# First attention of a decoder block: exponentials transposed by halves of the array, score strips read by 32 rows and 288 columns, contexts and side work spread over the steps

## Chip, cores and metric

The kernel runs on one NeuronCore of one Trainium2 chip. The metric is the device time of one execution in microseconds (us). Before the change three runs took 2130.73, 2132.78 and 2136.57 us; their median is 2132.78 us.

## What is computed

The reference is two transformer layers on x of 8 sequences x 512 tokens x 256 features, all in 32-bit floats: a disentangled attention with relative positions, a feed-forward layer with a low-rank part, a second attention over the sequences, and a mixture of 32 experts of which each token takes 4. Only the first attention is touched. It has 16 heads of 16 features:

```python
x = x + _L0_attn_ref(_layernorm(x))
...
scores = einsum('bhqd,bhkd->bhqk', q, k) / scale
c2p = take_along_axis(einsum('bhqd,hpd->bhqp', q, pos_k), clip(rel + 64, 0, 127))
p2c = swapaxes(take_along_axis(einsum('bhkd,hpd->bhkp', k, pos_k), clip(-rel + 64, 0, 127)))
probs = softmax(scores + (c2p + p2c) / scale)
ctx = einsum('bhqk,bhkd->bhqd', probs, v)
out = ctx @ Wo + bo + hidden
out = layernorm(out) * ln_scale + ln_bias
```

`rel` is a bucket of the distance between query and key. It changes only where the two are less than 128 tokens apart, so only a band of some 255 diagonals needs values of its own; outside the band the bucket is one of two constants.

## The kernel before

The first attention is the function `_l0_attention`. Its work is 256 steps: 8 sequences b, 4 groups g of four heads, 4 tiles i of 128 queries, and 2 pairs p of heads (L248). The order on every engine is the order in which the loop of L494 to L539 issues, since the schedule is manual (L486). One turn of the loop, for step n, does this:

- **Products** (L362). For both heads of the pair PE multiplies queries and keys into a score bank each (L371). A head has 16 features padded to 32 rows, so a matmul takes 32 rows of the array, and the matmuls of two heads stand in different row groups. There are two score banks, so a head's products wait until DVE has read the bank's last content.
- **Strips** (L306), for step n + 5 (`AHEAD`). PE multiplies 128 queries, and 128 keys, with the 256 possible positions of the band (L314), again in 32 rows. ACT copies the result to SBUF (L321). POOL works out what the tile's own 128 x 128 block needs beside it (`own`, L324). SP writes the strip, 4 x 128 rows of 255 values, to one of four DRAM buffers (L331). In the next turn SP reads it back with a row step of 511 values instead of 512, which shifts each row by one and turns positions into keys (`read`, L337 to L347): one transfer for the part by keys (`winp`), one for the part by queries (`winc`), each 128 partitions x 2 heads x 384 columns, or 256 where the tile is the first or last of the sequence. One turn later POOL adds `own` to the middle 128 columns of both (`add`, L351).
- **Near keys** (L379). PE transposes up to three 128 x 128 blocks of `winp` a head onto the scores (L383). Those of step n + 2 are the last that are needed.
- **Weights** (L393). DVE adds `winc` to the scores and takes each row's minimum (L397), and ACT makes the exponential (L400).
- **Turned** (L403). PE transposes the exponentials of step n - 1, four 128 x 128 blocks a head into one PSUM bank (L407), and DVE copies each bank to SBUF (L409).
- **Weigh** (L412), in every odd step. PE multiplies the transposed exponentials of four heads with the values: 16 matmuls, each of which is two instructions and takes 32 columns of the array (L418). After the last tile of an odd group ACT copies the contexts (L429), and `divide` is put in the list of side work.
- **Side work**: one piece a step. First what is `urgent`, the projections of the next group to queries and keys (L290); else the first of a list whose entries carry the first step in which they may run (`later`, L255): values (L273), normalizing and turning the next sequence (`normalized`, L152, and `turn`, L264), dividing (L447), and for the sequence before the output projection (`out`, L460), its mean and variance (`measure`, L469) and its normalization (`norm`, L472), which has twelve POOL operations of 256 columns (L475 to L477).

A transpose is a matmul whose stationary operand is the data, and whose moving operand is the identity. Every matmul of 32-bit floats that isn't a transpose shows as two instructions in the profile. The helper `_batch_norm_stats` (L47) takes mean and variance of a list of tiles on DVE (L53 to L56), and raises to the power -1/2 on POOL (L58). The lines named here are the ones that the prediction follows.

Of the kernel before, what the change touches and what calls it, by code (L numbers as in the profile page):

```python
# [12 lines left out]
F32 = mybir.dt.float32  # L13
# [8 lines left out]
P = 128  # L22
B, S, H = 8, 512, 256
# [37 lines left out]

def _normalize(nc, out, x, mv, rstd, i):
    nc.vector.tensor_scalar(out, x, mv[:, i, 0:1], rstd[:, i : i + 1], ALU.subtract, ALU.mult)  # L63


class _Evacuate:
# [24 lines left out]
def _l0_attention(nc, tc, a, x, ident, mhalf, carry, prefetch):  # L91
# [6 lines left out]
    with ExitStack() as ctx:  # L98
# [20 lines left out]
        with tc.tile_pool(name="a_pos", bufs=1) as pp:  # L119
# [32 lines left out]
            def normalized(pool, b):  # L152

                stats = []

                def measure():
                    stats.extend(_batch_norm_stats(nc, pool, [x[b][:, t, :] for t in range(NT)], 1e-5, mhalf))

                def norm():
                    for t in range(NT):  # L160
                        _normalize(nc, xns[b % 2][:, t, :], x[b][:, t, :], *stats, t)

                return measure, norm

            for f in normalized(pp, 0):
                f()


            def position_keys(lhsT, out):
# [61 lines left out]
        for v in vs:  # L231
            nc.gpsimd.memset(v, 0.0)

        winc = []
        for n in range(2 * NT):
            w = wp.tile([P, 2, S], F32, tag=f"winc{n}", name=f"winc{n}")
            nc.gpsimd.memset(w, 0.0)
            winc.append(w)

        ctx_ps = ps_c.tile([P, S], F32, tag="ctx", name="ctx_ps")  # L240

# [64 lines left out]
        def strips(u, between=None):  # L306


            b, g, i, p = steps[u]
            s = sm[b, g]  # L310
            pas = [ps_a.tile([P, S], F32, tag="psa", name="pa") for j in range(2)]
            for t, (src, pos) in enumerate(((s[0], posc), (s[2], posp))):
                for pa, rs in zip(pas, heads(p)):
                    nc.tensor.matmul(  # L314
                        pa[:, t * W : (t + 1) * W], src[rs, i * P : (i + 1) * P], pos[rs, g, :], start=True, stop=True
                    )
                if t == 0 and between is not None:
                    between()
            st = sb.tile([P, 4, W], F32, tag="strip", name="strip")
            for j in range(2):  # L320
                nc.scalar.copy(st[:, 2 * j : 2 * j + 2, :].rearrange("p t w -> p (t w)"), pas[j])  # L321

            own = sb.tile([P, 2, 2, P], F32, tag="own", name="own", bufs=3)
            nc.gpsimd.tensor_tensor(  # L324
                own,
                aside.unsqueeze(2).to_broadcast([P, 2, 2, P]),
                st[:, :, W - 1 : W].rearrange("p (j t) o -> p t j o", t=2).to_broadcast([P, 2, 2, P]),
                ALU.mult,
            )
            d = shift[u % NSHIFT]  # L330
            nc.sync.dma_start(  # L331
                bass.AP(d.tensor, d.offset + P + 1, [[2 * W, P], [2 * W * P, 4], [1, W - 1]]), st[:, :, : W - 1]
            )
            wc = winc[u % (2 * NT)]
            wk_ = sb.tile([P, 2, WIN], F32, tag="winp", name="winp", bufs=8)

            def read():  # L337
                lo, hi, c0, c1 = near(i)
                for t, dst in ((1, wk_[:, :, c0:c1]), (0, wc[:, :, lo * P : hi * P])):
                    nc.sync.dma_start(  # L340
                        dst,
                        bass.AP(
                            d.tensor,
                            d.offset + t * 2 * W * P + P + c0,
                            [[2 * W - 1, P], [4 * W * P, 2], [1, c1 - c0]],
                        ),
                    )  # L347
# [12 lines left out]
            wins[u] = wc, wk_  # L360
# [39 lines left out]
            nc.scalar.activation(e, e, AF.Exp, bias=low, scale=-1.0, accum_out=totals[b, g // 2][:, i, r : r + 1])  # L400
            return e

        def turned(e):  # L403
            et_ps = ps_t.tile([P, S], F32, tag="pst", name="et_ps")
            for m in range(NT):
                ms = slice(m * P, (m + 1) * P)
                nc.tensor.transpose(et_ps[:, ms], e[:, ms], ident)  # L407
            et = sb.tile([P, S], F32, tag="et", name="et", bufs=6)
            nc.vector.tensor_copy(et, et_ps)  # L409
            return et  # L410

        def weigh(n, ets):  # L412

            b, g, i, _ = steps[n]
            odd = g % 2 == 1
            for m in range(NT):
                for r, et in enumerate(ets):
                    nc.tensor.matmul(  # L418
                        ctx_ps[32 * r : 32 * r + 32, i * P : (i + 1) * P],
                        vs[b % 2][:, m, g % 2, g // 2 * 4 + r, :],  # L420
                        et[:, m * P : (m + 1) * P],
                        start=m == 0 and i == 0 and not odd,
                        stop=m == NT - 1 and odd,
                        skip_group_check=True,
                    )
            if i < NT - 1 or not odd:
                return
            c = sb.tile([P, S], F32, tag="c", name="c", bufs=2)
            nc.scalar.copy(c, ctx_ps)  # L429

            rec = sb.tile([P, NT, 8], F32, tag="rec", name="rec")
            nc.vector.reciprocal(rec, totals.pop((b, g // 2)))
            wide = sb.tile([P, NT, P], F32, tag="wide", name="wide", bufs=1)
            nc.gpsimd.tensor_copy(
                wide.rearrange("p i (r e) -> p i r e", e=HD), rec.unsqueeze(3).to_broadcast([P, NT, 8, HD])
            )
            later(3, partial(divide, b, c, wide))
            if g == NG - 1:
                out, measure, norm = finish(b)
                if b == B - 1:  # L440
                    rest.extend([*[partial(out, t) for t in range(NT)], measure, norm])
                else:
                    later(3, *[partial(out, t, misc, sb) for t in range(NT)])
                    later(9, partial(measure, misc, sb))
                    later(12, partial(norm, misc, sb))

        def divide(b, c, wide):  # L447
            spread = ps_m.tile([P, S], F32, tag="misc", name="spread")
# [6 lines left out]
        def finish(b):  # L455

            xn = xns[b % 2]
            stats = []

            def out(t, bank, pool):  # L460
                po = bank("po")
                for g in range(NC):
                    nc.tensor.matmul(
                        po[:, :H], cns[b][g][:, t * P : (t + 1) * P], wo[:, g, :], start=g == 0, stop=g == NC - 1
                    )
                nc.vector.tensor_tensor(xn[:, t, :], xn[:, t, :], po[:, :H], ALU.add)
                nc.gpsimd.tensor_tensor(xn[:, t, :], xn[:, t, :], rows["bo"], ALU.add)

            def measure(bank, pool):  # L469
                stats.extend(_batch_norm_stats(nc, pool, [xn[:, t, :] for t in range(NT)], 1e-7, mhalf))  # L470

            def norm(bank, pool):  # L472
                for t in range(NT):
                    _normalize(nc, xn[:, t, :], xn[:, t, :], *stats, t)
# [11 lines left out]
        with tc.manual_schedule():  # L486
# [7 lines left out]
            for now in range(len(steps) + 3):  # L494
                n = now
                if n < len(steps):
                    b, g, i, p = steps[n]
                    if (i, p) == (0, 0):
# [1176 lines left out]
```

## Time and profile before

| | us |
|---|---|
| median of three runs | 2132.78 |
| the profiled execution | 2132.52 |
| its span, from first to last instruction | 2130.7 |
| first attention, first product to the end of the last step | 56.1 to 1121.0 |
| PE, DVE, ACT, POOL busy over the span | 1963.5, 1393.8, 1104.7, 1138.3 |
| L407, transposes of exponentials, busy | 268.2 in 2048 instructions of 274 ns |
| L418, contexts, busy | 140.0 in 4096 instructions of 277 ns |
| L409, copies of the transposed, busy | 328.7 in 512 instructions of 683 ns |
| L397 and L400, minimum and exponential, busy | 333.2 and 365.7 |
| strip writes (L331) and reads (L340) | 256 of 510 KB, 256 of 384 KB, 256 of 256 KB |

In the profile, PE stands for matmuls and PEld for the loads of their stationary operands, which overlap with matmuls; SPq is the queue from which SP issues transfers. The ends of matmuls are modelled, so the distance between two starts says more than a duration. A line of the timeline gives start and length in us, then engine, line, operation and `out<-in`; in brackets stands how long the engine was idle before it, and what ended that. A name like `128*128 128x128` is the stationary operand's rows and columns, then the moving operand's.

### The profile page before, as it was taken

The numbers are of one execution on the slowest core, as the hardware profiler recorded it, in microseconds if no ns is written. First come the engines' busy times: TensorE is split into PE (matmuls) and PEld (weight loads), VectorE is DVE, ScalarE is ACT, GpSimd is POOL, SyncE is SP. The second block draws the span as 40 slices with busy tenths as digits, with TensorE's granted clock in tenths as the row PEclk, the third lists the DMA queues.
The fourth block names the chain that finished last, engine by engine and source line by source line (L and its number), as shares of the span: only waits on it lengthen the run. The fifth ranks groups of instructions, "written<-read, shape, count | busy, mean of one in ns | idle before, by whom it ended". The sixth has DMA issues, their size and how long they took to land.

```text
span 2130.7 us, 46004 instructions
## 1 busy us (share of the span) xinstructions
PE 1963.5 (92%) x15908; PEld 1415.5 (66%) x15908; DVE 1393.8 (65%) x3715; ACT 1104.7 (52%) x2366; POOL 1138.3 (53%) x1328
## 2 busy tenths in 40 slices
PE   7999999999999999999998999989988777499997
PEld 4777677777776777777775666645555445388886
DVE  3576776767767677686777555347876776356666
ACT  2776767667676766767662122244444333144443
POOL 5666766767667676676753111013544443355555
PEclk7999999999999999999999999999999987699999
DMA  8998989898898989989883544900111114556788
GB/s 273 316 293 275 283 278 299 271 290 282 269 299 276 277 280 282 295 270 293 275 283 93 165 142 126 87 0 29 46 40 43 49 42 167 198 166 209 253 259 268
DMA packets 388916, 444.21 MB, mean 208 GB/s; under 512 B 43344, under 2 KB 367952, under 8 KB 388688
## 3 DMA queue, kind: packets, MB, share of 16 engines
q1 hardware_dynamic: 373904, 401.93, 62.4%
q0 software_dynamic: 13824, 38.29, 4.9%
q8 instruction: 130, 2.13, 0.4%
q10 hardware_dynamic: 960, 1.05, 0.1%
q14 instruction: 98, 0.80, 0.1%
HBM read 238.99 MB, written 202.19 MB: 207 GB/s over the span
## 4 chain that ended last, share of the span: by engine, by line
PE 32%; DVE 10%; issue 4%; ACT 2%; SPq 1%; DMA 1%; POOL 1%; POOLq 0%; DVEq 0%; ACTq 0%
PE pge L1430 7%; PE po L674 5%; PE poe L1448 3%; PE ph L666 3%; PE pq L925 2%; PE ao L1015 2%; PE ptr L1422 2%; DVE prod L786 1%; PE pv L937 1%; DVE value L786 1%; PE po L1044 1%; SPq L1387 1%; PE ps L962 1%; DVE st L53 1%; DVE xn L63 1%
## 5 line engine op out<-in xcount | busy, mean ns | idle before, releaser
L397 DVE CUSTOM_DVE_ANT_0 e<-sc,winc 128x512 f32<-128x512 f32 x512 | 333.2, 688 | 293.9 <-PE sc L383 127.5
L400 ACT ACTIVATE e<-e,low 128x512 f32<-128x512 f32 x512 | 365.7, 716 | 110.1 <-DVE low L397 105.6
L324 POOL TENSOR_TENSOR own<-aside,strip 128x512 f32<-128x512 f32 x256 | 268.9, 1051 | 205.1 <-ACT strip L321 178.9
L321 ACT COPY strip<-pa 128x512 f32<-128x512 f32 x512 | 275.7, 592 | 185.7 <-issue 54.6
L371 PE MATMUL sc<-sm,sm 32*128 32x256 f32 (+3 forms) x1792 | 326.0, 439 | 19.2 <-DVE low L397 19.2
L409 DVE COPY et<-et_ps 128x512 f32<-128x512 f32 x512 | 328.7, 683 | 0.3 <-PE et_ps L407 0.2
L314 PE MATMUL pa<-pos,sm 32*128 32x256 f32 x2048 | 299.1, 407 | 1.7 <-ACT sm L298 1.0
L407 PE MATMUL et_ps<-ident,e 128*128 128x128 f32 x2048 | 268.2, 274 | 0.2 <-DVE et L409 0.2
L869 POOL DMA_INDIRECT rows<-pay,slot x128 | 141.9, 1109 | 233.0 <-issue 218.2
L371 PEld LDWEIGHTS sc<-sm,sm 32*128 32x128 f32 x1792 | 162.2, 184 | 130.3 <-DVE low L397 51.8
L407 PEld LDWEIGHTS et_ps<-ident,e 128*128 128x128 f32 x2048 | 234.3, 142 | 0.6 <-ACT e L400 0.4
L351 POOL TENSOR_TENSOR winp<-winp,own 128x256 f32<-128x256 f32 x256 | 186.9, 730 | 76.8 <-DMA winp<-shift 63.0
L869 POOL DMA_INDIRECT results<-y,r x160 | 156.8, 980 | 122.8 <-ACT y L1450 74.7
L351 POOL TENSOR_TENSOR winc<-winc,own 128x256 f32<-128x256 f32 x256 | 187.2, 731 | 40.0 <-DMA winc<-shift 37.4
L383 PE MATMUL sc<-ident,winp 128*128 128x128 f32 x1280 | 199.6, 285 | 5.8 <-DMA winp<-shift 5.8
L383 PEld LDWEIGHTS sc<-ident,winp 128*128 128x128 f32 x1280 | 136.4, 141 | 80.7 <-issue 59.6
L314 PEld LDWEIGHTS pa<-pos,sm 32*128 32x128 f32 x2048 | 179.8, 187 | 12.5 <-ACT strip L321 2.4
L58 POOL TENSOR_TENSOR rstd<-var,mhalf 128x4 f32<-128x4 f32 x40 | 44.8, 1121 | 249.3 <-DVE var L56 226.2
L1430 PE MATMUL pge<-store,rT 128*128 x640 | 168.2, 386 | 2.5 <-DVE rT L1424 0.9
L418 PE MATMUL ctx_ps<-et,v 128*32 128x128 f32 x4096 | 140.0, 277 | 0.2 <-DVE et L409 0.2
L669 ACT ACTIVATE hT<-ph,b 128x512 f32<-128x512 f32 x64 | 44.0, 687 | 166.0 <-PE ph L666 166.0
L290 PE MATMUL pq<-xnT,wqk 128*128 128x512 f32 x256 | 126.0, 614 | 3.1 <-DVE xnT L78 3.1
(216 smaller groups left out, 3337.3 us busy)
## 6 DMA issues: line engine op xcount, KB each, us to landing
shift<-strip SPq DMA_DIRECT2D x256, 510.0 KB
winp<-shift SPq DMA_DIRECT2D x128, 384.0 KB
winc<-shift SPq DMA_DIRECT2D x128, 384.0 KB
winp<-shift SPq DMA_DIRECT2D x128, 256.0 KB
winc<-shift SPq DMA_DIRECT2D x128, 256.0 KB
rows<-empty SPq DMA_DIRECT2D x8, 2640.0 KB
r<-rows SPq DMA_DIRECT2D x160, 132.0 KB
z<-results SPq DMA_DIRECT2D x32, 512.0 KB
```

The lines of the kernel that those rows point to most:

```text
L314: nc.tensor.matmul(pa[:, t * W : (t + 1) * W], src[rs, i * P : (i + 1) * P], pos[rs, g, :], start=True, stop=True)
L321: nc.scalar.copy(st[:, 2 * j : 2 * j + 2, :].rearrange("p t w -> p (t w)"), pas[j])
L324: nc.gpsimd.tensor_tensor(own, aside.unsqueeze(2).to_broadcast([P, 2, 2, P]), st[:, :, W - 1 : W].rearrange("p (j t) o -> p t j o", t=2).t ...
L351: nc.gpsimd.tensor_tensor(dst, dst, own[:, t], ALU.add)
L371: nc.tensor.matmul(sc[:, c0:c1], s[side_][rs, cut : cut + P], s[2 + side_][rs, c0:c1], start=c0 == 0, stop=False, skip_group_check=True,)
L383: nc.tensor.matmul(sc[:, m * P : (m + 1) * P], wins[n + 2 * (m - i)][1][:, j, (i - m + 1) * P : (i - m + 2) * P], ident, start=False, stop ...
L397: nc.vector.tensor_tensor_reduce(e, sc, wins[n][0][:, j, :], 1.0, -LOW, ALU.add, ALU.min, low)
L400: nc.scalar.activation(e, e, AF.Exp, bias=low, scale=-1.0, accum_out=totals[b, g // 2][:, i, r : r + 1])
L407: nc.tensor.transpose(et_ps[:, ms], e[:, ms], ident)
L409: nc.vector.tensor_copy(et, et_ps)
L869: ins = nc.gpsimd.indirect_dma_start(to, bass.IndirectOffsetOnAxis(ap=index, axis=0), source, None, bounds_check=last)
L1430: nc.tensor.matmul(pg[:, :H], rT[:, k * P : (k + 1) * P], w[:, k * H : (k + 1) * H], start=k == 0, stop=k == NK - 1)
```

## The change

It has four parts.

1. **Transposes by halves.** `turned` takes both heads of a step. Each 128 x 128 block of exponentials is transposed as two blocks of 64 rows, which take the upper and the lower half of the array's rows and go to two PSUM banks, in turn. Each of the two banks holds one half of the queries of both heads; DVE copies each bank as before. 8 transposes a step become 16, of 64 moving columns instead of 128.
2. **Strips read by 32 rows.** Each of the two reads becomes four, of 32 partitions. A row of the band needs only 255 columns, and 32 rows that are shifted against each other need 32 + 255, so each transfer reads 288 columns instead of 384 (fewer at the sequence's ends). The tiles that are read into are now permanent and cleared once at the start, since the columns outside the 288 have to stay zero; the tiles for `winc` of different query tiles share memory. The strip gets a third buffer.
3. **Contexts in every step.** `weigh` is done in two halves, half of the keys in an odd step and the other half in the even one after it.
4. **Side work in smaller pieces.** `measure` and `norm` handle two tiles at a time instead of four, and their pieces get earlier or other places in the list.

```diff
+def _measure(nc, pool, stats, tiles, eps, mhalf):
+    stats.append(_batch_norm_stats(nc, pool, tiles, eps, mhalf))
...
-                def measure():
-                    stats.extend(_batch_norm_stats(nc, pool, [x[b][:, t, :] for t in range(NT)], 1e-5, mhalf))
...
+                def measure(t):
+                    _measure(nc, pool, stats, [x[b][:, i, :] for i in (t, t + 1)], 1e-5, mhalf)
+
+                def norm(t):
+                    for i in range(2):
+                        _normalize(nc, xns[b % 2][:, t + i, :], x[b][:, t + i, :], *stats[t // 2], i)
+
+                return [partial(f, t) for f in (measure, norm) for t in (0, 2)]
...
+        winc, winp = [None] * (2 * NT), []
+        for p in range(2):
+            for i, width in ((0, S + 2 * P), (1, S + 3 * P)):
+                w = wp.tile([P, 2, width], F32, tag=f"winc{i}{p}", name="winc")
+                nc.gpsimd.memset(w, 0.0)
+                winc[2 * i + p], winc[2 * (NT - 1 - i) + p] = w[:, :, :S], w[:, :, width - S :]
         for n in range(2 * NT):
-            w = wp.tile([P, 2, S], F32, tag=f"winc{n}", name=f"winc{n}")
+            w = wp.tile([P, 2, WIN], F32, tag=f"winp{n}", name="winp")
             nc.gpsimd.memset(w, 0.0)
...
-            st = sb.tile([P, 4, W], F32, tag="strip", name="strip")
+            st = sb.tile([P, 4, W], F32, tag="strip", name="strip", bufs=3)
...
-            wk_ = sb.tile([P, 2, WIN], F32, tag="winp", name="winp", bufs=8)
+            wk_ = winp[u % (2 * NT)]
 
             def read():
-                lo, hi, c0, c1 = near(i)
-                for t, dst in ((1, wk_[:, :, c0:c1]), (0, wc[:, :, lo * P : hi * P])):
-                    nc.sync.dma_start(
-                        dst,
-                        bass.AP(
-                            d.tensor,
-                            d.offset + t * 2 * W * P + P + c0,
-                            [[2 * W - 1, P], [4 * W * P, 2], [1, c1 - c0]],
-                        ),
-                    )
+
+                lo, hi, first, end = near(i)
+                for t, dst, o in ((1, wk_, 0), (0, wc, (i - 1) * P)):
+                    for p0 in range(0, P, 32):
+                        c0, c1 = max(first, p0), min(end, p0 + 2 * P + 32)
+                        nc.sync.dma_start(
+                            dst[p0 : p0 + 32, :, o + c0 : o + c1],
+                            bass.AP(
+                                d.tensor,
+                                d.offset + t * 2 * W * P + P + c0 + p0 * (2 * W - 1),
+                                [[2 * W - 1, 32], [4 * W * P, 2], [1, c1 - c0]],
+                            ),
+                        )
...
-        def turned(e):
-            et_ps = ps_t.tile([P, S], F32, tag="pst", name="et_ps")
-            for m in range(NT):
-                ms = slice(m * P, (m + 1) * P)
-                nc.tensor.transpose(et_ps[:, ms], e[:, ms], ident)
-            et = sb.tile([P, S], F32, tag="et", name="et", bufs=6)
-            nc.vector.tensor_copy(et, et_ps)
-            return et
+        def turned(es):
+
+
+            banks = [ps_t.tile([P, S], F32, tag="pst", name="et_ps") for _ in range(2)]
+            for j, e in enumerate(es):
+                for m in range(NT):
+                    for f, bank in enumerate(banks):
+                        rs, c = slice(64 * f, 64 * f + 64), (j * NT + m) * 64
+                        nc.tensor.transpose(bank[:, c : c + 64], e[rs, m * P : (m + 1) * P], ident[rs, rs])
+            et = sb.tile([P, 2, 2, NT, 64], F32, tag="et", name="et", bufs=4)
+            for f, bank in enumerate(banks):
+                nc.vector.tensor_copy(et[:, f].rearrange("p j m q -> p (j m q)"), bank)
+            return [et[:, :, j] for j in range(2)]
...
-        def weigh(n, ets):
+        def weigh(n, ets, part):
...
-            for m in range(NT):
+            for m in range(2 * part, 2 * part + 2):
...
-                        et[:, m * P : (m + 1) * P],
+                        et[:, :, m, :],
...
-            if i < NT - 1 or not odd:
+            if part == 0 or i < NT - 1 or not odd:
                 return
-            c = sb.tile([P, S], F32, tag="c", name="c", bufs=2)
+            c = sb.tile([P, S], F32, tag="c", name="c", bufs=1)
...
+                fs = [*[partial(out, t) for t in range(NT)], *[partial(f, t) for f in (measure, norm) for t in (0, 2)]]
                 if b == B - 1:
-                    rest.extend([*[partial(out, t) for t in range(NT)], measure, norm])
+                    rest.extend(fs)
                 else:
-                    later(3, *[partial(out, t, misc, sb) for t in range(NT)])
-                    later(9, partial(measure, misc, sb))
-                    later(12, partial(norm, misc, sb))
+                    later(3, *[partial(f, misc, sb) for f in fs])
...
+                        if g == NG - 3 and b + 1 < B:
+                            ready = normalized(sb, b + 1)
+                            later(4, *ready[:2])
                         if g == NG - 2 and b + 1 < B:
-                            measure, norm = normalized(sb, b + 1)
-                            later(1, measure)
-                            later(3, norm, *[partial(turn, b + 1, k) for k in range(NK)])
+                            later(2, *ready[2:], *[partial(turn, b + 1, k) for k in range(NK)])
...
-                        ets.extend(turned(e) for e in es)
+                        ets.extend(turned(es))
...
-                    weigh(n - 3, [ets.popleft() for _ in range(4)])
+                    four = [ets.popleft() for _ in range(4)]
+                    weigh(n - 3, four, 0)
+                elif n % 2 == 0 and n >= 4:
+                    weigh(n - 4, four, 1)
```

`measure` and `norm` of the output get the same form in `finish`.

More of the change, by code (lines that the diff above doesn't have):

```diff
@@ L154, in normalized @@
                 stats = []
-                def measure():
-                    stats.extend(_batch_norm_stats(nc, pool, [x[b][:, t, :] for t in range(NT)], 1e-5, mhalf))
[L159 to L166, printed above, removed]
+                def measure(t):
[4 more added lines that the diff above has]
+                return [partial(f, t) for f in (measure, norm) for t in (0, 2)]
+            ready = normalized(pp, 0)
+            for n in (0, 2, 1, 3):
+                ready[n]()
             def position_keys(lhsT, out):
@@ L232, in _l0_attention @@
             nc.gpsimd.memset(v, 0.0)
-        winc = []
+        winc, winp = [None] * (2 * NT), []
[4 more added lines that the diff above has]
+                winc[2 * i + p], winc[2 * (NT - 1 - i) + p] = w[:, :, :S], w[:, :, width - S :]
         for n in range(2 * NT):
-            w = wp.tile([P, 2, S], F32, tag=f"winc{n}", name=f"winc{n}")
+            w = wp.tile([P, 2, WIN], F32, tag=f"winp{n}", name="winp")
             nc.gpsimd.memset(w, 0.0)
-            winc.append(w)
+            winp.append(w)
         ctx_ps = ps_c.tile([P, S], F32, tag="ctx", name="ctx_ps")
@@ L467, in out, with measure, norm @@
                 nc.gpsimd.tensor_tensor(xn[:, t, :], xn[:, t, :], rows["bo"], ALU.add)
[L469 to L474, printed above, removed]
+            def measure(t, bank, pool):
+                _measure(nc, pool, stats, [xn[:, i, :] for i in (t, t + 1)], 1e-7, mhalf)
+            def norm(first, bank, pool):
+                for t in (first, first + 1):
+                    _normalize(nc, xn[:, t, :], xn[:, t, :], *stats[first // 2], t - first)
                     nc.gpsimd.tensor_tensor(xn[:, t, :], xn[:, t, :], rows["ln_scale"], ALU.mult)
```

## Prediction

> **What bounds the kernel now.** I read the busy table by stage first, then the timeline of single steps, then the waits, then SP's own rows. The change touches the first attention alone: 256 steps between 56.1 and 1121.0 us of a 2130.7 us span, 4.16 us a step.
>
> ```profile
> core 0: us, PE busy (x) PEld busy (x) DVE busy (x) ACT busy (x) POOL busy (x), PEclk, DMA share, GB/s
> 56.10:1121.00 1064.90, 1035.77 (x11781) 774.47 (x11780) 752.08 (x1854) 738.53 (x1672) 725.79 (x902) 0.99 0.91 284
> ```
>
> PE is busy 97% of the stage, DVE, ACT and POOL about 70%; the DMA engines stand at 91%. The timeline of one step (time, us, engine, line, tiles) says what PE's time is made of:
>
> ```profile
> 603.98 0.19 PEld L371 LDWEIGHTS sc<-sm,sm 32*128 32x128 f32 x2 [0.20 <-issue]
> 603.99 0.19 PEld L314 LDWEIGHTS pa<-pos,sm 32*128 32x128 f32 x2
> ...
> 604.75 0.38 PE L314 MATMUL pa<-pos,sm 32*128 32x256 f32 x2
> 605.05 0.64 PEld L383 LDWEIGHTS sc<-ident,winp 128*128 128x128 f32 x6 [0.33 <-issue]
> 605.06 0.87 PE L383 MATMUL sc<-ident,winp 128*128 128x128 f32 x6
> ...
> 605.66 0.91 PEld L407 LDWEIGHTS et_ps<-ident,e 128*128 128x128 f32 x8
> 605.77 1.04 PE L407 MATMUL et_ps<-ident,e 128*128 128x128 f32 x8
> ```
>
> Four things are to be seen. (a) Eight transposes at L407 take 1.04 us, of which the last is 0.27: one starts every (1.04-0.27)/7 = 0.110 us. (b) Four loads of 32 rows, two at L371 and two at L314, start within 0.01 us and all last 0.19: loads in different row groups run side by side. (c) L383 to L407 costs nothing (605.06 + 6 x 0.109 = 605.71 against 605.77, the rest being the first load), but the last L314 pair starts at 604.75, needs 0.21 (its neighbours start 0.21 apart) and L383 starts only at 605.05: 0.09 us lost where the shape of the array changes. L407 to L418 (last start 602.77, +0.11, L418 at 602.97) and L418 to L371 show 0.09 too. (d) The two loads ahead of a first transpose, looked at alone:
>
> ```profile
> 605.05 0.20 PEld L383 LDWEIGHTS sc<-ident,winp 128*128 128x128 f32 x2 [0.33 <-issue]
> ```
>
> One lasts 0.14, two 0.20: a load in a transpose needs about 0.057 us, so today's 0.110 is set by the 128 columns of identity that stream, not by the load.
>
> ```profile
> PEld sc L371 <- DVE low L397: 51.8, 137, 1.4
> ...
> PE sc L371 <- DVE low L397: 19.2, 28, 1.2
> ```
>
> These waits (us, times, longest) are short steps that catch up with DVE: the next products need the score bank that DVE's L397 still reads. SP's rows (min/median/max ns):
>
> ```profile
> L340 SPq DMA_DIRECT2D winp<-shift x256: 359/447/1676, 44.5 to 1107.6; - x128
> L340 SPq DMA_DIRECT2D winc<-shift x256: 359/927/1522, 44.9 to 1108.1; - x128
> ...
> L599 SPq DMA_DIRECT2D token_rows<-xn x8: 319/324/338, 1104.6 to 1319.4; - x8
> ```
>
> An issue costs SP 0.36 us at least, and a 16-row one at L599 still 0.32: the cost hardly depends on the rows.
>
> **What the Trainium skill says.** "TensorE: Matmul & The Clock Gate", Part 3: weight loads overlap running matmuls only when the row group differs; the trace agrees (b). "TensorEngine Tiling (Array Packing)", Key Properties: a change of tiling mode drains the array; the trace agrees at 0.09 us. "SBUF — State Buffer", Door 1: partitions 0..31 reach 8 of 16 DMA ports and measured 189 GB/s; "DMA: Bandwidth & Descriptors", Rules for kernel authors: two transfers to disjoint partition halves serialize. No run here shows either; today's strip reads go to 128 partitions.
>
> **The change, part by part** (us a step; times 256 for the stage).
>
> Halved transposes. Removed: 8 x 0.109 = 0.87. Added: 16 of 64 rows and 64 columns. Streaming is 0.109/2 = 0.055; the load, still 128 columns, 0.057; the halves are two row groups and two banks, so 8 pairs x 0.057 = 0.46, plus a new change of shape after L383 (0.09) and its uncovered first load (0.055): 0.60. Net -0.27, -68 us. Bounds: streaming alone, 8 x 0.055, gives -0.28; no overlap, 16 x 0.057 + 0.15 = 1.06, gives +0.19. I take -0.27. DVE's two copies (L409, 0.68 each) are unchanged, and come after L397 in DVE's order anyway.
>
> Contexts by halves. The same 32 matmuls, in every step instead of every second. A step is quiet when no side work runs on PE in it. Odd quiet steps exceed even ones (2.75) by 1.01 where no wait is in them, of which 8 sets of four x 0.107 = 0.86 stream; entering costs about 0.14, now also in 128 even steps: +18. Where side work on PE follows in an even step, it now comes from another shape (today's steps from 85.44 to 89.70 and on to 95.16, both with a projection, differ by 5.46 - 4.26 = 1.20, about 0.20 more than the quiet ones): 20 of a batch's 32 steps have such work (8 projections, 4 values, 4 outputs, 2 divides, 2 turns), half of them even, 80 x 0.20 = +16.
>
> Evenness. Quiet steps today alternate 4.24 (from 97.91 to 102.15) and 2.75 (on to 104.91); 0.47 of the pair, 0.24 a step, is the wait for DVE. Afterwards a quiet step needs 2.75 - 0.27 + 0.43 + 0.14 = 3.05 of PE. But there is a loop: from the first near key (605.06) to the end of the second L397 2.09, 0.07 to the next products, 1.07 from there to the next near key: 3.23. PE work that is taken out of a quiet step below this only turns into that wait, so 0.18 of it stays; (0.24 - 0.18) x 96 quiet steps = -6.
>
> Measures and norms by halves. Steps with them run over today; against the sums of their PE work a batch loses about 5 us. What a norm issues stays: four L63 on DVE (0.72 to 0.78 each), for the output's norm also twelve POOL operations (L475 to L477, 0.74 each, 8.9 in all); each measure now makes two L58 on POOL, 1.1 each, instead of one. The halves follow each other in successive quiet steps, where POOL already has own and two adds, 2.5 of 3.2. So POOL catches up hardly sooner: behind the norm stand the next strip's own (L324) and the adds (L351), and the near keys wait for those. I take -1 a batch, -8; bounds 0 and -40.
>
> Reads. Bytes: today 768 KB inside and 512 at the edges, mean 640; after, 32 rows x 288 columns give 576, the clipped edges (mean 208 columns) 416, mean 496. With the 510 KB write that is 1.03 MB instead of 1.18; at 284/0.91 = 312 GB/s 3.3 us a step instead of 3.8. DMA isn't what PE waits for (L383 for DMA: 14 us in all), so this is worth about nothing directly. Price: 9 issues instead of 3. SP: 9 x 0.36 + 0.08 of semaphores = 3.3 us a step, under the mean step, 0.1 over a quiet one. Behind the eight reads stands the next strip's write; POOL's adds wait for four landings each instead of one, with the next own behind them, and the near keys two steps on wait for the adds. Strips run five steps ahead, so long steps pay back what SP loses in short ones: +4. PE's extra semaphore waits are hidden behind its queue, as two per step at L407 are now.
>
> Third strip buffer, persistent winp tiles, one c: 0, since ACT's strips start 0.09 us after PE's last L314 ends, and so wait for PE. POOL's memsets grow from 8 x 1024 to 12,800 elements a partition, at 0.95 us per 1024 by 4.3 us, in 9.8 us of POOL's idle time before 40.12; without that cover +4. The last half of the contexts comes one step later: +1.
>
> Sum: -68 + 18 + 16 - 6 - 8 + 4 + 1 = -43. The profiled execution took 2132.5 (span 2130.7 and 1.8 around it), 0.3 under the median of 2132.8; 2132.5 - 43 is **2090**.
>
> **Rivals.**
> (1) Slower: the **DMA engines become the bound**, since a 32-row read reaches half the ports. At the page's 189 GB/s the mean 0.51 MB of reads takes 2.69 us, the write 0.52 MB/312 = 1.67, semaphores 0.08: 4.44 against 4.16 now, +0.28 x 256 = +72: 2205. It decides from 4.16 - 1.75 = 2.41, i.e. reads under 211 GB/s. For: 91% today. Against: neighbouring reads alternate between port halves, and packets of several reads are in flight together.
> (2) **SP becomes the bound**: today's medians are 0.45 and 0.93, waiting for a full DMA queue. At 0.45 a step is 9 x 0.45 + 0.08 = 4.13, 0.03 under today: 2125. It decides from 0.43: 9 x 0.43 + 0.08 = 3.95 is about my mean step after (4.16 - 43/256 = 3.99).
> (3) The **halves don't overlap** (the change doesn't do what it says): (1.06 - 0.60) x 256 = 118 on the forecast, 2208. Against it is (b).
> (4) **More is won**: the bursts vanish (-32 more) and the lighter DMA takes away the few long stalls in which DVE stood for winp (28.4 us): 2030.
>
> **How the numbers follow.** Forecast 0.50, (1) 0.18, (2) 0.13, (3) 0.06, (4) 0.13. A measurement of this kernel tells about 0.3% from no change, 6 us. Forecast and (4) are faster, and half of (2); a third of (2) is within: faster 0.69, same 0.05, slower 0.26. The forecast's own range is 2062 (the bursts gone) to 2112 (half of the change's gain lost to SP). The wide range takes in (2), most of (4) and the milder half of (1), at which the halves are partly used together: 2045 to 2190; some 2 in 10 are left out, the rest of (1) and (4), and (3).
>
> **What would show it.** Right: L407 pairs every 0.057 us, 0.46 a step; 0.09 between L383 and L407; quiet steps of 3.2; L418 in every step; SP's read issues at 0.36. Wrong: L407 starts 0.057 apart one by one (3); SP's reads at 0.45 and more with PE's L383 waiting for winp (2); the DMA share over 0.95 with fewer GB/s (1). Any of these makes the forecast wrong.

## The result and the profile after

The changed kernel takes **2408.9 us** (2407.0 to 2411.7), against 2132.2 for the kernel before beside it: a ratio of 1.1295, 95% interval [1.1275, 1.1315]. The forecast was 2090 with a range of 2045 to 2190; the kernel became 277 us slower, and the sign was wrong. Its profiled span is 2406.8 us, and nearly all of the difference lies in the stage that the change touches. A step there now takes 5.24 us on average (from the first product of step 0 to that of step 255) instead of 4.16. First the same table of the stage as shown for the kernel before:

```profile
core 0: us, PE busy (x) PEld busy (x) DVE busy (x) ACT busy (x) POOL busy (x), PEclk, DMA share, GB/s
56.80:1397.00 1340.20, 1093.90 (x13805) 734.59 (x13804) 746.22 (x1867) 738.83 (x1672) 734.69 (x916) 0.90 0.74 198
```

PE was busy 97% of the stage and is now busy 82%; DVE, ACT and POOL do the same work in a longer time; the DMA engines have fallen from 91% to 74% and from 284 to 198 GB/s. So no engine of this table is the bound. The waits of the stage (us, times, longest) say what PE and POOL lack:

```profile
POOL winp L365 <- DMA winp<-shift: 238.3, 174, 6.1
PE sc L397 <- DMA winp<-shift: 234.5, 93, 9.3
```

The near keys (L397) and the adds (L365) wait for windows that haven't landed, while the DMA engines stand idle for a quarter of the time: the transfers come late because they are *asked for* late. Who asks is SP. Its timeline in the kernel before (start, us, line; x1 is one issue):

```profile
501.63 0.36 SPq L331 DMA_DIRECT2D shift<-strip  x1
502.09 0.45 SPq L340 DMA_DIRECT2D winp<-shift  x1
502.63 0.94 SPq L340 DMA_DIRECT2D winc<-shift  x1
505.39 0.36 SPq L331 DMA_DIRECT2D shift<-strip  x1
```

and in the changed kernel:

```profile
499.77 0.38 SPq L342 DMA_DIRECT2D shift<-strip  x1
500.25 2.38 SPq L354 DMA_DIRECT2D winp<-shift  x4
502.74 1.77 SPq L354 DMA_DIRECT2D winc<-shift  x4
504.61 0.38 SPq L342 DMA_DIRECT2D shift<-strip  x1
```

Before, SP issues for 1.9 us and then waits 1.8 us for the next strip. Now one issue follows the other without a pause, and the step is as long as the nine issues: 504.61 - 499.77 = 4.84 here. The rows of SP's reads, and its waits in the stage before and after, say the same:

```profile
SPq L331 <- ACT strip L321: 478.2, 249, 4.1
```

```profile
L354 SPq DMA_DIRECT2D winp<-shift x1024: 302/438/2500, 44.6 to 1384.0; - x171
L354 SPq DMA_DIRECT2D winc<-shift x1024: 302/425/2135, 46.4 to 1385.9; - x171
...
SPq L342 <- ACT strip L332: 9.1, 29, 0.9
```

SP used to wait 478 us for strips; now 9. (Each `x1024` row holds all reads into one of the two windows, four a step; its three numbers are the shortest, the median and the longest issue in ns.) The medians, 0.44 and 0.43, are not yet the whole price. Sorted by their place after the write (100 to 1000 us, mean us), the nine issues take 0.40 (the write), 0.46, **0.97**, 0.46, 0.43, 0.43, 0.51, 0.47 and 0.46, in sum 4.6; between them lie gaps of about 0.06, 0.52 a step, and the semaphore instructions take 0.07. Together 5.2 of a 5.26 us step: **SP is the bound.**

PE doesn't lose this time evenly. The 32 first steps of a group of heads (tile 0, first pair) last 383 us in sum, 12.1 in the median, where the kernel before takes 141 and 4.25: 242 of the 277 us that were lost lie there. The near keys of tile 3 need no window of a later tile, so PE works on while SP falls behind; the next tile 0 needs one that stands three further on in SP's order than any that PE has needed so far, and there PE has to wait until SP has caught up:

```profile
728.93 0.87 PE L397 MATMUL sc<-ident,winp 128*128 128x128 f32 x3 [5.48 <-DMA winp<-shift]
729.74 1.12 PE L425 MATMUL et_ps<-ident,e 64*128 64x64 f32 x16
```

The halved transposes themselves, by contrast, are as forecast (start, us):

```profile
504.33 0.63 PE L397 MATMUL sc<-ident,winp 128*128 128x128 f32 x4 [1.16 <-DMA winp<-shift]
504.89 0.71 PE L425 MATMUL et_ps<-ident,e 64*128 64x64 f32 x16
505.54 0.64 PE L437 MATMUL ctx_ps<-et,v 128*32 128x128 f32 x16
```

Sixteen take 0.65 from the first start to the first context, where eight took 0.96 to 0.97 (448.08 to 449.05 in the kernel before), and pairs start 0.06 apart. The bracket on the first line is a wait for a window, in the middle of a step.

### The profile page after: what moved, and what is told of

It reads as the page before. It is cut to its first block, busy times and chain, and to the rows that moved or that the text cites. A ratio compares the mean times of both kernels' runs of the same rounds, so it can differ in the third digit from the quotient of the medians.

```text
span 2406.8 us, 52429 instructions
## 1 busy us (share of the span) xinstructions
PE 2021.8 (84%) x17956; PEld 1377.3 (57%) x17956; DVE 1385.8 (58%) x3731; ACT 1104.9 (46%) x2366; POOL 1151.3 (48%) x1348
## 3 DMA queue, kind: packets, MB, share of 16 engines
q10 hardware_dynamic: 960, 1.05, 0.1%
## 4 chain that ended last, share of the span: by engine, by line
PE 32%; DVE 9%; SPq 6%; DMA 5%; issue 4%; POOL 2%; ACT 2%; another core or an unknown queue 0%; POOLq 0%; DVEq 0%; ACTq 0%
PE pge L1452 5%; PE po L696 5%; SPq L354 4%; DMA winp<-shift 3%; PE poe L1470 3%; PE ph L688 3%; PE ao L1037 1%; PE pq L947 1%; PE ptr L1444 1%; DVE prod L808 1%; PE sc L397 1%; PE sc L385 1%; PE et_ps L425 1%; PE ctx_ps L437 1%; PE pv L959 1%
## 5 line engine op out<-in xcount | busy, mean ns | idle before, releaser
L397 PE MATMUL sc<-ident,winp 128*128 128x128 f32 x1280 | 231.5, 302 | 234.8 <-DMA winp<-shift 234.5
L397 PEld LDWEIGHTS sc<-ident,winp 128*128 128x128 f32 x1280 | 144.5, 149 | 329.7 <-issue 190.4
L365 POOL TENSOR_TENSOR winp<-winp,own 128x256 f32<-128x256 f32 x256 | 185.7, 725 | 301.5 <-DMA winp<-shift 238.3
L365 POOL TENSOR_TENSOR winc<-winc,own 128x256 f32<-128x256 f32 x256 | 186.4, 728 | 254.6 <-DMA winc<-shift 221.8
L325 PE MATMUL pa<-pos,sm 32*128 32x256 f32 x2048 | 305.4, 417 | 1.7 <-ACT sm L309 1.0
L385 PEld LDWEIGHTS sc<-sm,sm 32*128 32x128 f32 x1792 | 167.6, 191 | 111.8 <-issue 47.9
L425 PE MATMUL et_ps<-ident,e 64*128 64x64 f32 x4096 | 199.6, 243 | 1.1 <-DVE et L428 1.1
L425 PEld LDWEIGHTS et_ps<-ident,e 64*128 64x128 f32 x4096 | 162.3, 151 | 50.6 <-issue 36.9
L437 PE MATMUL ctx_ps<-et,v 128*32 128x128 f32 x4096 | 184.6, 304 | 0.5 <-DVE et L428 0.5
L58 POOL TENSOR_TENSOR rstd<-var,mhalf 128x2 f32<-128x2 f32 (+1 forms) x56 | 51.2, 915 | 229.2 <-DVE var L56 207.1
L301 PE MATMUL pq<-xnT,wqk 128*128 128x512 f32 x256 | 158.2, 748 | 0.1
L309 ACT ACTIVATE sm<-pq,bias 128x512 f32<-128x512 f32 x128 | 80.8, 683 | 121.8 <-PE pq L301 115.3
```

Of the source, the lines that this page charges most:

```text
L325: nc.tensor.matmul(pa[:, t * W : (t + 1) * W], src[rs, i * P : (i + 1) * P], pos[rs, g, :], start=True, stop=True)
L385: nc.tensor.matmul(sc[:, c0:c1], s[side_][rs, cut : cut + P], s[2 + side_][rs, c0:c1], start=c0 == 0, stop=False, skip_group_check=True,)
L397: nc.tensor.matmul(sc[:, m * P : (m + 1) * P], wins[n + 2 * (m - i)][1][:, j, (i - m + 1) * P : (i - m + 2) * P], ident, start=False, stop ...
L425: nc.tensor.transpose(bank[:, c : c + 64], e[rs, m * P : (m + 1) * P], ident[rs, rs])
```

## The experiments

The theory after the result: the PE side of the forecast stands, and the loss is SP's issuing, at some 0.58 us an issue with its gap instead of the 0.36 forecast. The rival is the forecast's rival (1): not the issues cost the time, but the transfers themselves. All ratios are to the kernel before, run beside each kernel; a difference in us is the difference of ratios times 2132. E9 to E11 ran on another chip, where the kernel before took 2145.4 us, so only their ratios can be set beside the others. A transfer's *rows* are its contiguous pieces, one for each partition and head: 64 in a 32-partition read, 256 in a whole read, 512 in the write.

**E1, whole reads.** The changed kernel with the two reads of a step by all 128 rows again:

```diff
-                    for p0 in range(0, P, 32):
-                        c0, c1 = max(first, p0), min(end, p0 + 2 * P + 32)
-                        nc.sync.dma_start(
-                            dst[p0 : p0 + 32, :, o + c0 : o + c1],
...
+                    nc.sync.dma_start(
+                        dst[:, :, o + first : o + end],
```

> The changed kernel with its strip reads put back to one transfer of 128 rows each (384 columns, 256 at the ends), so SP issues 3 transfers a step instead of 9; halved transposes, split contexts and side work stay. Theory A (SP's issues are the bound of the changed kernel: 9 a step at 0.53 us and 0.06 between them are 5.2 us): SP falls to under 2 us a step, PE is the bound again, and what the prediction summed for the other parts is left, 2090 us (2070 to 2110). Theory B (32-row transfers are slow in the DMA engines[...]): also about 2090, since those are gone too. Theory C (the halved transposes or the order of side work cost the time): over 2200 us.

Measured: 2107.3 us, 0.9888 [0.9858, 0.9917]. Everything but the reads together gains 24 us; the reads cost 300. That the transfers themselves were slow isn't excluded by this run, since they are gone too. The stage's table is back to the form of before:

```profile
56.10:1094.00 1037.90, 1006.45 (x13806) 693.32 (x13805) 755.50 (x1868) 740.08 (x1673) 727.96 (x916) 1.00 0.93 291
```

**E2, reads by 64 rows.** As the change, with `range(0, P, 64)` and 320 columns: five issues a step.

> The changed kernel with reads of 64 rows and 320 columns: 4 reads a step instead of 8[...]. Theory A: SP issues 5 transfers, about 2.9 us a step, less than PE needs; 2090 to 2115 us. Theory B: [...]4.6 us a step, 2250 us or more.

Measured: 2129.9 us, 0.9994 [0.9973, 1.0014], a little above my range and far below theory B, which is the forecast's rival (1) again. Five issues don't cost five ninths: the reads of 64 partitions (128 rows) take 0.57 to 0.60 each in the median back to back where those of 32 partitions took 0.43. SP is at 3.8 of a 4.15 us step: just short of the bound.

**E3, six more issues.** The kernel before, with six transfers of 64 rows of four values each behind the reads, into tiles that nobody uses. They add 6 KB to a step's 1.2 MB:

```diff
+                for _ in range(6):
+                    spare = sb.tile([32, 2, 4], F32, tag="spare", name="spare", bufs=64)
+                    nc.sync.dma_start(
+                        spare, bass.AP(d.tensor, d.offset, [[2 * W - 1, 32], [4 * W * P, 2], [1, 4]])
+                    )
```

> The kernel before, with six transfers of 32 rows x 2 x 4 values (16 bytes each row) added on SP after the two reads of each step, into tiles that nothing reads. They add 6 KB a step, and no work elsewhere. Theory A: SP needs 1.7 us for what it does now, and 6 x 0.43 us and 0.06 between them more, 4.9 to 5.0 us a step against 4.16: 2320 us (2250 to 2400). Theory B: nothing but 6 KB more, 2132 to 2145 us.

Measured: 2452.3 us, 1.1503 [1.1475, 1.1531]. That is above even theory A's range: six issues that move next to nothing cost as much as the changed reads. The bytes aren't needed for such a loss. How much of it is SP's issuing this run alone doesn't say: E7 finds a second limit that holds it too.

**E4, the reads alone.** The kernel before with the 32-row reads and nothing else of the change.

> The kernel before with the reads by 32 rows and 288 columns alone (and the permanent winp tiles that they need); whole transposes, contexts in odd steps, two strip buffers. Theory A: SP's 5.2 us a step stay the bound, so about the changed kernel's time, 2400 us (2370 to 2450), the other parts hidden behind SP. Theory C: between 2132 and 2200, the loss being in the other parts.

Measured: 2394.0 us, 1.1234 [1.1205, 1.1263], as expected. Even on the slower PE side of the kernel before, SP sets the step: its issues, gaps and semaphore instructions are 5.17 of 5.20 us.

**E5, halved transposes alone.** The kernel before with `turned(es)` of the change.

> The kernel before with the transposes by halves alone; reads, contexts and side work as before. Theory A (the step costs what its TensorE work costs, and the halves save 0.27 us of it): 256 steps x 0.27 = 69 us less, 2064 us (2055 to 2080). Theory B (a saving on TensorE comes back as waits for the strips or in the bursts of side work): 2085 to 2110. If the halves had shared the array badly it would be above 2132.

Measured: 2123.1 us, 0.9952 [0.9936, 0.9969]: 10 us of the 69. Where the rest went can be read in one quiet pair of steps, the last two of a group. The kernel before:

```profile
447.59 0.66 PE L383 MATMUL sc<-ident,winp 128*128 128x128 f32 x4
448.08 1.04 PE L407 MATMUL et_ps<-ident,e 128*128 128x128 f32 x8
449.05 1.17 PE L371 MATMUL sc<-sm,sm 32*128 32x384 f32 x3
```

and E5, its PE, and its DVE in the same stretch:

```profile
441.38 0.66 PE L383 MATMUL sc<-ident,winp 128*128 128x128 f32 x4
441.98 0.71 PE L411 MATMUL et_ps<-ident,e 64*128 64x64 f32 x16
442.82 1.20 PE L371 MATMUL sc<-sm,sm 32*128 32x384 f32 x3
```

```profile
442.07 0.69 DVE L397 CUSTOM_DVE_ANT_0 e<-sc,winc 128x512 f32<-128x512 f32 x1 [1.17 <-DMA winp<-shift]
442.69 0.08 DVE L397 DVE_READ_ACCUMULATOR2_ANT low<- 128x1 f32 x1
```

From the first near key to the next step's products it was 1.46 us and is 1.44. The transposes are done sooner, but the products may write the score bank only when DVE's L397 has read it, at 442.77. In the odd step, where the contexts stand between, the same stretch went from 2.48 to 2.24. Over all steps, those that got shorter gained 23 us, 17 of it in odd steps. Others, nearly all of them in groups 1 and 2, where the measures and norms still come in one piece, gave 15 back: the odd steps at tile 2 of group 2 went from a median 4.96 to 6.18.

**E6, contexts at once.** E1 with both halves of the contexts in the odd step, as before.

```diff
                     weigh(n - 3, four, 0)
-                elif n % 2 == 0 and n >= 4:
-                    weigh(n - 4, four, 1)
+                    weigh(n - 3, four, 1)
```

> The whole-read version of the changed kernel with both halves of a pair's contexts in one odd step, as before. Theory A (the second entry into contexts costs 0.14 us in 128 steps, and context matmuls beside side work cost another 0.2 us in 80 steps, as forecast): 2107 - 34 = 2073 us (2065 to 2085). Theory B (spreading contexts over both steps is worth its extra entry): 2107 to 2125.

Measured: **2087.3 us, 0.9791** [0.9767, 0.9816], the fastest of all. The split contexts cost 21 us here. In quiet pairs they do what the forecast says, 2.88 + 3.12 against 2.52 + 3.92 at the end of a group; they lose in pairs with side work, most in the last pair of group 2, where 9.58 stands against 7.02. One wait of 1.39 there is E1's PE waiting for DVE to copy a turned tile; I did not take the rest of the 2.56 apart. The wait:

```profile
409.56 0.66 PE L466 MATMUL spread<-ident,wide 128*128 128x128 f32 x4 [1.39 <-DVE xnT L82]
```

**E7, six issues of one row.** E3 with transfers of one row of four values, `[[2 * W - 1, 1], [1, 4]]`.

> The kernel before with six dummy transfers of one row of 4 values on SP's queue in each step (the earlier dummies had 64 rows of 4 values, cost 0.425 us each and gave 2452). Theory A (an issue costs SP about 0.28 us and 2.3 ns for each row it describes, from 0.425 us for 64 rows and 0.575 us for 128): six cost 6 x 0.34 = 2.0 us with the gaps, SP's step comes to about 3.7 us, below the 4.16 of the kernel before: 2132 to 2165 us. Theory B (an issue costs 0.43 us whatever it describes): 2440 to 2460 again.

Measured: 2364.9 us, 1.1087 [1.1069, 1.1106]: between my two theories, and for a reason that neither had. The issues are cheap, as theory A says:

```profile
L351 SPq DMA_DIRECT2D spare<-shift x1536: 214/250/468, 44.2 to 1342.1; - x192
```

but SP waits, and not for a strip or a window's reader:

```profile
SPq L331 <- DMA winp<-shift: 182.5, 232, 2.7
SPq L340 <- DMA winc<-shift: 99.2, 178, 2.2
```

The operands of the issues explain it. Each names a semaphore that it raises and waits for that same semaphore first; there are eight of them, used in turn. So an issue waits until the transfer eight issues back has landed, that is, has raised its semaphore for the last time. At three issues a step that is some 2.7 steps ago. At nine it is less than one: the first read of a step waits for the second read of the step before, which stands half a microsecond after its own first read and lands 4.5 us after its issue (median): a cycle of 5.0, and E7's step is 5.08. The write starts 0.06 us after the landing it waits for in at least three of four steps. In the changed kernel this second limit is hardly reached: at each of the nine places the issues start a median 0.98 us or more after that landing (0.39 or more at the 5th percentile). In E3 it is: in half of its steps the first read starts within 0.07 us of the landing, and its cycle, 4.7 from issue to landing and 0.5 between the two reads, comes to 5.2 of its 5.45. So E3 mixes both limits, and the case for SP's issuing rests on E4, E8 and the sums of SP's time below.

**E8, two queues.** The changed kernel with the four reads into winc issued from ScalarE.

```diff
-                        nc.sync.dma_start(
+                        (nc.sync if t else nc.scalar).dma_start(
```

> The changed kernel with the four reads into winc issued from ScalarE instead of SP; the same transfers, bytes and rows. Theory A (SP's own issuing is the limit): SP is left with five issues, about 2.8 us a step, and ScalarE gets 4 x 0.43 = 1.7 us on top of some 2.85, about 4.6 us a step with its waits: 2230 to 2330. Theory B (the limit lies behind the queues, in the transfers or in something that both queues share): 2390 or more.

Measured: 2255.4 us, 1.0554 [1.0522, 1.0586], in the range of theory A: a step of 4.64, forecast 4.6. The same bytes to the same partitions come 158 us sooner when another queue does four of the nine issues. What ScalarE pays for them is a median 0.44 each, a mean 0.48:

```profile
L354 ACTq DMA_DIRECT2D winc<-shift x1024: 309/437/2208, 44.1 to 1229.8; - x171
```

ScalarE now computes or issues for 4.3 of the 4.64 us of a step.

SP's accounts in all of these (100 to 1000 us of each, us a step; gaps up to 0.15 us counted with the issues, longer ones as waits; while SP waits, as in E3 and E7, rows of the last issue may still be being worked off, which then shows in no issue):

| kernel | issues | rows | SP issuing, with gaps | SP waiting | step |
|---|---|---|---|---|---|
| before | 3 | 1024 | 1.96 | 2.22 | 4.19 |
| E1 | 3 | 1024 | 1.99 | 2.08 | 4.07 |
| E2, 64 rows | 5 | 1024 | 3.79 | 0.36 | 4.15 |
| E4, 32 rows | 9 | 1024 | 5.17 | 0.03 | 5.20 |
| after | 9 | 1024 | 5.23 | 0.03 | 5.26 |
| E3 | 9 | 1408 | 4.94 | 0.51 | 5.45 |
| E7 | 9 | 1030 | 3.50 | 1.58 | 5.08 |
| E8, SP alone | 5 | 768 | 2.99 | 1.65 | 4.64 |

**E9, side work alone.** The kernel before with measures and norms by halves and their new due times, and with the change's layout of the window, strip and context tiles.

> The kernel before with the new side work (measures and norms by halves, earlier and spread) and the new tile layout of the windows alone; whole reads, 128-row transposes, contexts at once. Added last, to a kernel with halved transposes, these were worth 36 us (2123 to 2087). Theory A (they are worth that by themselves): 2133 - 36 = 2097 us (2085 to 2107). Theory B (they give free what the halves had saved and the bursts took back, and little alone, as the 14 us of the forecast say): 2112 to 2130.

Measured: 2120.0 us, 0.9881 [0.9854, 0.9908], 25 us less than the kernel before beside it; on the 2133 of the theories that is 2108, just above theory A's range. The side work gains by itself, and 9 us more beside halved transposes, which is little more than the three ratios can tell (some 8 us). The crowded steps are those that shrink (medians, us): tile 2 of group 2, even step, 4.93 to 3.77; group 1, tiles 2 and 3, even, 3.68 to 2.75 and 3.78 to 2.99; group 2, tile 0, odd, 6.11 to 5.46.

**E10, split contexts alone.** The kernel before with the contexts over both steps (`weigh` of the change).

> The kernel before with the contexts of a pair of steps split over both steps alone. Theory A (the split costs its second entry and its place beside side work, 20 us as with whole reads): 2153 us (2143 to 2165). Theory B (it evens odd and even steps, and gains more than the entries cost as long as the transposes are long): 2105 to 2133.

Measured: 2159.7 us, 1.0070 [1.0048, 1.0093], +15 us, theory A. Quiet pairs gain (2.53 + 4.13 to 3.11 + 3.12 at the end of a batch), pairs with a projection or an output lose (4.26 + 5.46 to 5.03 + 5.03; 3.62 + 3.77 to 4.39 + 4.39 in tile 1 of group 1).

**E11, contexts put off only into quiet steps.** E6 with a choice:

```diff
-                    weigh(n - 3, four, 1)
+                    due = len(urgent) + sum(at <= n + 1 for at, _ in side)
+                    put_off = due <= 1 and (n + 1) % (2 * NT) != 0
+                    if not put_off:
+                        weigh(n - 3, four, 1)
+                elif n % 2 == 0 and n >= 4 and put_off:
+                    weigh(n - 4, four, 1)
```

> The version with contexts at once (2087 us), in which the second half of a pair's contexts is put off to the next, even step only where no side work is due there. By pairs of steps, the split version is shorter in (0,1), (0,2), (1,2), (2,2) and (3,3) of group and tile, by 0.43, 0.78, 0.60, 0.43 and 0.44 us, and longer in the others. Theory A (each pair keeps the shorter of its two times): 8 x 2.7 = 21 us less, 2066 us (2060 to 2076). Theory B (pairs depend on their neighbours, and time saved in one is waited for in the next): 2080 to 2090.

Measured: 2110.6 us, 0.9838 [0.9820, 0.9856], by the ratios some 10 us slower than E6, and slower than both theories had it. Theory A fell. Some quiet pairs did get shorter, but the last step of group 2 took 5.65, near E1's 5.51, where E6 has 4.13, and tile 1 of group 1 took 3.58 + 4.60 where E6 has 3.58 + 3.54. Times of pairs can't be picked from two kernels and added. What ties a pair to its neighbours here I did not test further.

## Why the prediction was wrong

**The step that failed: "Price: 9 issues instead of 3. SP: 9 x 0.36 + 0.08 of semaphores = 3.3 us a step."** It rested on "An issue costs SP 0.36 us at least, and a 16-row one at L599 still 0.32: the cost hardly depends on the rows." Both readings were of issues that an SP with free time made. The write shows how little they say: its 512 rows keep SP 0.40 us, a read of 64 rows soon behind it 0.97. Only an issue right behind others shows the whole price, and the same row of the profile had it: medians of 447 and 927 ns at L340. I put those down to a full DMA queue, and left them out of the forecast's price. Measured, a read of the changed kernel costs a mean 0.52 and a gap of 0.06, so nine issues and the semaphores 5.2 us a step and not 3.3. And rows do count: an issue back to back takes 0.25 for one row (E7), 0.43 for 64 (E3, E8), 0.57 to 0.60 for 128 (E2), 2.5 to 3 ns a row on top of 0.25. For 64 rows it is the same whether a row has 16 bytes (E3) or 640 to 1152 (E8). The 0.9 of the second issue after the write fits a write whose 512 rows are still being worked off, which the traces show only by the pattern. The line doesn't carry to the write's rows: for all of E3's it would give 9 x 0.25 + 1408 x 0.0025 = 5.8 us, more than its whole step of 5.45. And no run here separates whether the time for rows goes into describing them or into a queue behind SP that takes them at this pace; it isn't the bytes.

**"Strips run five steps ahead, so long steps pay back what SP loses in short ones: +4."** This holds only where SP's mean is under PE's. At 5.2 against 4.0 there is no time to pay back with; the term became +300. The lead was shorter than five, too: the turn of step n issues the read for step n + 4, and its near keys need the window of n + 2.

**Rival (2)** named the right bound, and its threshold of 0.43 an issue was crossed. But it priced an issue at 0.45 from one median, without the gaps between issues and without the long second issue. "0.03 under today" was a warning: a price that lands on the threshold needed both ends, and the 0.93 in the same row, carried over to one issue in nine, would have given 0.08 + 0.36 + 7 x 0.45 + 0.93 + 9 x 0.06 = 5.06, or 0.90 x 256 = 230 more: 2362.

**Rival (1)**, the ports ("SBUF — State Buffer", Door 1, in the Trainium skill), isn't what set the time: E8 gains 158 us with the same bytes and partitions. Whether 32-row reads would reach a limit of their own near its 4.44 us a step, no run shows, since ScalarE alone fills 4.3 of E8's 4.64.

**Rival (3)** fell by the trace: pairs start 0.06 apart. But what the prediction read from (b) goes less far than it says. (b) shows loads beside loads, in different row groups. The loads at L407 all take 128 rows, and yet from the second on each starts 1 or 2 ns after a transpose has started and runs beside it (eight loads from 605.66 to 606.57, eight transposes from 605.77 on), so "only when the row group differs" isn't what this trace shows.

**The PE terms** came out at 24 us together where the forecast had 47 (E1), but not by their parts:

| part | forecast us | measured alone us |
|---|---|---|
| halved transposes | -68 | -10 (E5) |
| contexts split, with evenness | +18 + 16 - 6 | +15 (E10); +21 on top of the rest (E6 to E1) |
| measures and norms by halves | -8 | -25 (E9); -34 on top of E5 (E6) |
| reads | +4 | +263 (E4); +300 on top of the rest |

(The measured rows are runs of their own, with the buffers that each needed, so they needn't add up; the third contains the new layout of the tiles.) The operations' prices were right: 0.24 saved on the transposes where no wait follows, for the 0.27 forecast; quiet steps of 3.10 and 3.23 in E1, for the 3.23 of the loop. What was mis-sized is what a saving on PE is worth. I charged the loop through DVE once, against the evened steps, but in even quiet steps it already stood right behind the transposes (E5). With the side work I saw that "a batch loses about 5 us" and took 1 of it, for POOL's sake; E9 shows some 3.

## What to carry to other kernels

Before you cut one transfer into several, add up the issuing queue's time for a step at the price of issues that follow each other without a pause, gaps and rows included, and compare it with the step: fewer bytes bought with more issues lost 300 us here. Durations of issues that were read while the queue had time to spare were a lower bound here (0.36), not the price when it was full (0.52 and a gap). And price a saving on the busiest engine at the first thing that waits behind it: of the 68 us that the halved transposes save in PE's work, 10 reached the kernel's time alone, and some 20 beside thinned-out side work.

## What the runs showed that I had not expected

- Transfers here go through eight semaphores in turn, and an issue waits for the transfer eight back. Where the second whole read landed 4.5 us after its issue, that alone held nine issues a step at about 5.0 us (E7), though issuing was cheaper.
- An issue's price has a part per row: 0.25, 0.43 and 0.58 us for 1, 64 and 128 rows. Going from nine issues to five at the same number of rows (E2 against the change) took SP from 5.23 to 3.79 a step.
- Where PE had to wait in these runs, its granted clock was lower: 1.00 in E1's stage, 0.90 in the changed kernel's. PE waits for over 4 us 28 times in the changed kernel's stage, and in each of these waits a stretch at half clock begins; E1's stage has one such wait and one such stretch. After the wait of 5.48 shown above the clock stands at 0.54 from 729.0 to 735.1: the sixteen transposes take 1.05 us to the first context instead of 0.65, and four projection matmuls (L301) 3.29 to the next products, where the kernel before takes 1.81 (L290, 353.82 to 355.63). So PE's stall cost it more than the stall's own length. Whether that cost the kernel any time no run shows, since SP set the step.
